# A second weight matrix read in pieces for each tile, more buffers for activations, residual and probabilities, and q ahead of o in an attention and LoRA kernel

## The chip, the core and the metric

The kernel runs on one core of one Trainium2 chip. Its engines are TensorE (PE in the profile, with its weight loads as PEld), VectorE (DVE), ScalarE (ACT), GpSimd (POOL) and SyncE (SP), which here only issues DMAs. Each has a queue of its own that it works off in order, and waits on semaphores for the others. The metric is the device time of one execution in microseconds (us).

## What is computed

The input x has 4 sequences of 512 tokens with 1024 features, in float32. Two blocks follow each other, each with a layer norm in front, a layer norm behind and a residual:

```python
x = x + layernorm(attention(layernorm(x)))
x = x + layernorm(ffn(layernorm(x)))

def attention(x):            # 32 heads of 32, 8 heads of k and v, causal
    q, k, v = split(x @ w_qkv.T + b_qkv)
    q, k = rope(q), rope(k)
    scores = where(causal, q @ k.T / sqrt(32), -1e20)
    return (softmax(scores) @ v) @ w_o.T + b_o

def ffn(x):                  # a dense layer and the two best of 8 LoRA experts
    w = softmax over the two largest of x @ gate_w.T, 0 for the others
    low = x @ lora_A[e].T    # 16 numbers for each expert
    return x @ base_w.T + base_b + 2 * sum_e w[e] * low[e] @ lora_B[e].T
```

## The kernel before

The 2048 tokens make 16 tiles of 128. A tile's position in its sequence is i = 0 to 3; its tokens attend to i + 1 blocks of 128 keys. Tile 12 (i = 0 of the last sequence) gives its k and v in its turn, but its q, attention and ffn come last of all (`line`, L584; job "12q", L586). All weights are loaded once and stay in SBUF: w_qkv, w_o, w_gl (gate and lora_A side by side), w_base, w_lora (lora_B).

For each tile the work is this.

- `load_x` (L591) loads x in two halves into the one buffer "xa"; `qkv` (L628) normalises it, turns it with TensorE (pt_xn) into T_xn, and multiplies: kv (8 steps over the 1024 features), q in two halves of 512 columns (8 steps each). A step of 512 columns is one product of 128x128 by 128x512, which the profile shows as two MATMULs. k and q are rotated (`rotated`, L506) and turned (pt_k, pt_q).
- Attention goes by groups of up to 4 heads for each of the 4 row quadrants of the array (`Group`, L1000; i = 0, 1, 2, 3 make 2, 4, 8, 8 groups for a tile). `scores` (L1011) fills one PSUM tile sc; VectorE adds the mask and takes the maximum (L1079, L1089), ScalarE takes the exponential (L1039), VectorE the reciprocal of its sum (L1048), GpSimd multiplies by it (L1053). `turn` (L1098) turns the four probability tiles (pt_p) and has them copied to prT; `values` (L1116) multiplies them by v (av). The result is put together in aT.
- `attention_out` (L768) multiplies aT by w_o (acc_o, two halves of 8 steps), adds b_o into w, normalises it, adds it to y (x of the same tile, loaded again by `load_y`, L613), and normalises y into w once more: that is h.
- `ffn` (L874) turns h (pt_h, T_h), multiplies by w_gl (acc_gl), weighs the experts (`gate`, L832), turns their 128 numbers (pt_low), and multiplies by w_base and w_lora (acc_f: two halves of 8 + 1 steps). Bias, norm and residual follow, and y goes out in two halves (L949).

What sets the order of the instructions on each engine is a planner in Python that runs while the kernel is built (`Order`, L89). It keeps an estimated time for every operation. Chains (Python generators) yield operations for VectorE, ScalarE, GpSimd or SP with a duration and an urgency (0 first); `_next` (L138) takes the most urgent that is ready, and one that is more urgent and will be ready within half the operation's time is waited for. TensorE's work stands in lanes (`tensor`, L232): the scores, the transposes of xn, h, q, k and low, the lane of pt_p and values, and the dense lanes (q and kv, o, gl and f of each tile). `_choice` (L198) takes the first lane, in this order, whose next step is ready. Among dense lanes those that have begun go first (`lane[0].bank` is false once a product has its PSUM bank), then they go in the order of the list, which L1224 to L1236 builds: for n = 0, 1, ... o of tile n-2, q and kv of tile n, then gl and f of tile n-2.

Buffers are `Slots` (L50): a chain asks for one and goes on when one is given back. The ones that the change touches:

```python
BANKS, SOFT = 4, 8
soft_slots, act_slots = Slots(SOFT), Slots(3)
xa_slots, y_slots, w_slots = Slots(1), Slots(1), Slots(2)
```

`act_slots` (three buffers "actT") hold T_xn from before its transposes to the end of q, aT from q's arrival to the end of o, and T_h from the first half of h to the end of f. T_xn also waits until the tile before it in `line` has taken its aT (`job.after`, L1192). `soft_slots` hold the probabilities pr and prT. `y_slots` has one buffer, which is given back when y has gone out to HBM; the last tile's y lies in the buffer "xa" instead, once the last x is turned (L665). All loads and stores are issued by SP in the planner's order, the weights in the sequence of `all_loads` (L1150), where w_base comes after w_o and w_gl in 8 chunks of 512 KB.

The last tile's two attention groups g0 and g1 are placed by hand (L1203 to L1205): g1 at the very end, g0 three places before the end of the list at that time, with two groups of tile 15 and then g1 behind it.

Of the kernel before, what the change touches and what calls it, by code (L numbers as in the profile page):

```python
# [11 lines left out]
F32 = mybir.dt.float32  # L12
# [4 lines left out]
P = 128  # L17
# [6 lines left out]
QUADS = P // HD  # L24
# [64 lines left out]
class Order:  # L89
# [48 lines left out]
    def _next(self):  # L138

        best = None  # L140
        for e in self.ENGINES:
            ops = self.waiting[e]
            if not ops:
                continue
            start = max(self.free[e], min(op.ready for op in ops))
            op = min(
                (op for op in ops if op.ready <= start + 1e-9), key=lambda op: (op.urgent, op.seq)
            )
            us = op.on[e][0]
            sooner = [  # L150
                o for o in ops if o.urgent < op.urgent and o.ready < start + us / 2
            ]
            if sooner:
                op = min(sooner, key=lambda o: (o.ready, o.seq))
                start = max(self.free[e], op.ready)
            if best is None or start < best[0]:
                best = (start, e, op)
        return best
# [101 lines left out]
def kernel(  # L260
# [26 lines left out]
    QSCALE = 1.0 / math.sqrt(HD)  # L287
    BANKS, SOFT = 4, 8

    const = ctx.enter_context(tc.tile_pool(name="const", bufs=1))  # L290
    xpool = ctx.enter_context(tc.tile_pool(name="xpool", bufs=1))
    acts = ctx.enter_context(tc.tile_pool(name="acts", bufs=3))
    ropes = ctx.enter_context(tc.tile_pool(name="ropes", bufs=1))
    qpool = ctx.enter_context(tc.tile_pool(name="qpool", bufs=3))
    kvpool = ctx.enter_context(tc.tile_pool(name="kvpool", bufs=3))
    soft = ctx.enter_context(tc.tile_pool(name="soft", bufs=SOFT))
    small = ctx.enter_context(tc.tile_pool(name="small", bufs=2))
    ps_sc = ctx.enter_context(tc.tile_pool(name="ps_sc", bufs=1, space=PSUM))
# [4 lines left out]
    banks = Slots(BANKS)  # L303
    soft_slots, act_slots = Slots(SOFT), Slots(3)
    qT_slots, kT_slots, raw_slots, turn_slots = Slots(3), Slots(3), Slots(2), Slots(1)
    xa_slots, y_slots, w_slots = Slots(1), Slots(1), Slots(2)
    order = Order(banks)
# [47 lines left out]
    wgl_sb = const.tile([P, ND, GL], F32, name="wgl_sb")  # L355
    wbase_sb = const.tile([P, ND, D], F32, name="wbase_sb")
    wlora_sb = const.tile([P, D], F32, name="wlora_sb")
# [21 lines left out]
    def loads(what):  # L379


        def lands(name):
            yield LANDS
            loaded[name].finish(order.at)

        for name, kb, out, in_ in what:
            yield sp(kb / RATE, lambda: nc.sync.dma_start(out=out, in_=in_))
            start(lands(name), order.at)


# [88 lines left out]

    def project(lhsT, w_sb, at, n, name, needs, take, more=None):  # L480

# [4 lines left out]
        def issue(c):  # L486
            if not acc:
# [4 lines left out]
                lhsT=lhsT()[:, c, :] if c < ND else more[0](),  # L492
                rhs=w_sb[:, c, at : at + n] if c < ND else more[1][:, at : at + n],
                start=(c == 0),
# [96 lines left out]
    def load_x(job):  # L591
# [5 lines left out]
        rows = slice(job.tok.t * P, (job.tok.t + 1) * P)  # L597
        job.xn = xpool.tile([P, D], F32, tag="xa", name=f"xa_{job.name}")

# [13 lines left out]
    def load_y(tok):  # L613

        last = tok.last
        yield (xa_slots if last else y_slots).take()
        yield has_wqkv

        def issue():
            tag = "xa" if last else "y"  # L620
            tok.y = xpool.tile([P, D], F32, tag=tag, name=f"y_{tok.t}")
            nc.sync.dma_start(out=tok.y, in_=x[tok.t * P : (tok.t + 1) * P, :])

        yield sp(P * D * 4 / 1024 / RATE, issue)
        yield LANDS
        tok.has_y.finish(order.at)

    def qkv(job, has_k, has_q):  # L628
# [33 lines left out]
        def free_x():  # L662
            yield [s.done for s in turns]
            xa_slots.give(order.at)
            if job is jobs[-1]:  # L665
                start(load_y(line[-1]), order.at)

# [80 lines left out]
        if has_k:  # L748
            products += project(
                xnT, wqkv_sb, D, 2 * KVD, f"kv_{t}", needs(D, 2 * KVD), take_kv  # L750
            )
            turned.append(step_k)
        if has_q:
            for h in range(NH):
                products += project(
                    xnT,
                    wqkv_sb,
                    h * 512,
                    512,
# [8 lines left out]
    def attention_out(tok):  # L768
# [52 lines left out]
        for h in range(NH):  # L821
# [5 lines left out]
            steps += project(  # L827
                lambda: tok.aT, wo_sb, h * 512, 512, f"o_{t}_{h}", needs, partial(take, h)
            )
# [44 lines left out]
    def ffn(tok):  # L874
# [81 lines left out]
        def rest():  # L956
# [7 lines left out]
            yield out_halves  # L964
            if not tok.last:
                y_slots.give(order.at)

        start(rest())

        def needs(name, at, more=()):  # L970
            return [
                [ready[c // 4]] + ([loaded[name, at, c]] if not t else []) for c in range(ND)
            ] + list(more)

        gl = project(
            hT,
            wgl_sb,
            0,
            GL,
# [3 lines left out]
        )  # L983
        f = [
            project(
                hT,
                wbase_sb,
                n * 512,
                512,
                f"f_{t}_{n}",  # L990
                needs("base", 0, [[tok.low_done] + ([loaded["lora"]] if not t else [])]),
                partial(take, n),
                more=(lambda: tok.lowT, wlora_sb),
            )
            for n in range(NH)
        ]
        return turns, gl + f[0][:ND] + f[1][:2] + f[0][ND:] + f[1][2:], [step_low]
# [13 lines left out]
    def scores(g):  # L1011
# [18 lines left out]

        def quadrant(r):
            yield soft_slots.take()
            pr = soft.tile([P, GROUP, P], F32, tag="soft", name=f"pr_{g.name}_{r}")
            pr = g.pr[r] = pr.rearrange("p a b -> p (a b)")
            for c in range(g.n):
                yield act(
                    0.42 + n * 0.00092,
                    1,
                    lambda: nc.scalar.activation(  # L1039
# [9 lines left out]
            for c in range(g.n):  # L1049
                yield pool(  # L1050
                    0.3 + n * 0.00085,
                    1,
                    lambda: nc.gpsimd.tensor_scalar(  # L1053
# [93 lines left out]

    has_wk, has_wqkv = Task(), Task()

    def all_loads():  # L1150
# [7 lines left out]
        for c in range(ND):  # L1158
# [6 lines left out]
            ]  # L1165
            + chunks("base", wbase_sb, w_base, 0, D)
            + [
# [5 lines left out]
        def chain():  # L1173
# [5 lines left out]
            has_wqkv.finish(order.at)  # L1179
            yield from loads(late)  # L1180

        start(chain())
# [6 lines left out]
    for n, job in enumerate(jobs):  # L1189
        at = line.index(job.tok) if job.has_q else n  # L1190

        job.after = line[at - 1] if at > 2 else line[0] if at == 2 else None  # L1192
        start(load_x(job))
    for tok in line[:-1]:
        start(load_y(tok))
# [7 lines left out]
    *groups, g0, g1 = groups  # L1203
    groups.insert(len(groups) - 0, g1)
    groups.insert(len(groups) - 3, g0)  # L1205
    for k, g in enumerate(groups):
# [17 lines left out]
    for n in range(T + 2):  # L1224

        if n > 1:
            dense_lanes.append(attention_out(line[n - 2]))
        while n < T and left and (left[0].tok.t <= line[n].t or n == T - 1):
# [3 lines left out]
            dense_lanes.append(dense)  # L1232
        if n > 1:
            turns, dense, turn_low = ffn(line[n - 2])
            turn_lanes += [turns, turn_low]
            dense_lanes.append(dense)  # L1236
    order.tensor(score_lane, turn_lanes, value_lane, dense_lanes)

# [76 lines left out]
```

## Time and profile before

| what | value |
|---|---|
| time, 3 runs | 1246.52 us median (1245.53 to 1246.68) |
| the profiled execution | 1246.57 us, of it 1244.7 us from the first to the last instruction |
| TensorE's granted clock, mean | 0.991 |
| acc_f, matmuls with w_base | 512 MATMULs 128x512, 236.0 us busy, mean 593 ns |
| acc_o | 512 MATMULs 128x512, 233.2 us busy, mean 593 ns |
| pt_p | 1280 MATMULs, 178.9 us busy; idle before them 13.5 us |
| DMA, whole execution | 44.69 MB, mean 36 GB/s |
| w_base loads | 8 of 512 KB, 9.8 us from issue to landing (median) |

"Busy" is the time in which an engine had at least one instruction under way; MATMULs are pipelined, so that their own durations overlap, and 12 of 128x512 take 5.15 us together. "Idle before" is the time in which the engine had nothing under way ahead of such an instruction, and its releaser is the instruction that ended the wait. In the slices the span is cut into 40 equal parts, with the busy share in tenths. In a table of stages each engine's busy time is followed by its number of instructions. "PEq" or "SPq" is an engine's queue.

### The profile page before, as it was taken

Reading aid. Unit: us, or ns where it says so; the run is one execution under the profiler, and the core shown is the slowest. Engines: PE = TensorE matmul, PEld = TensorE weight load, DVE = VectorE, ACT = ScalarE, POOL = GpSimd, SP = SyncE. Lnnn points to the kernel's source line nnn. Section 1 sums busy time; section 2 is a strip of 40 time slices with the busy share of each in tenths; the row PEclk is TensorE's granted clock in tenths of the full one; section 3 lists DMA queues with packets and bytes.
Section 4 is the critical chain, followed back from the end, with each engine's and each line's share of the span. In section 5 each row is a group of like instructions: output and inputs, shape, how many; then the busy total and the mean of one; then the engine's idle time right before and its main releaser. Section 6 shows DMA issues by size and latency. Waiting matters only on the chain.

```text
span 1244.7 us, 19839 instructions
## 1 busy us (share of the span) xinstructions
PE 1212.1 (97%) x7416; PEld 659.6 (53%) x7416; DVE 807.8 (65%) x1678; ACT 430.2 (35%) x1355; POOL 450.6 (36%) x696
## 2 busy tenths in 40 slices
PE   6999999999999999999999999999999999987997
PEld 3555545555555555555555555555555555544553
DVE  3657657668566766767656766667566676566653
ACT  0343433433444343433322323334433333343300
POOL 1343434143352433435332524324334242334311
PEclk9999999999999999999999999999999999997999
DMA  9800000010010101000100101010010010100000
GB/s 335 319 2 18 1 35 18 2 51 1 18 35 1 52 1 35 18 25 11 35 17 18 35 1 51 2 51 18 1 52 1 1 52 1 52 1 1 15 20 34
DMA packets 18655, 44.69 MB, mean 36 GB/s; under 512 B 2432, under 2 KB 3456, under 8 KB 18560
## 3 DMA queue, kind: packets, MB, share of 16 engines
q1 hardware_dynamic: 18560, 43.43, 9.9%
q8 instruction: 59, 0.97, 0.3%
q14 instruction: 36, 0.29, 0.1%
HBM read 35.03 MB, written 8.39 MB: 35 GB/s over the span
## 4 chain that ended last, share of the span: by engine, by line
PE 96%; DVE 2%; ACT 0%; POOL 0%; DMA 0%; issue 0%; POOLq 0%; SPq 0%; ACTq 0%
PE acc_f L490 20%; PE acc_o L490 18%; PE acc_q L490 17%; PE pt_p L1103 12%; PE acc_kv L490 9%; PE sc L1019 7%; PE av L1126 6%; PE acc_gl L490 2%; PE pt_h L465 1%; PE pt_q L721 1%; PE pt_xn L465 1%; DVE nmax L1089 0%; PE pt_k L690 0%; ACT pr L1039 0%; DMA xa<-in_x_dram 0%; DVE stats L405 0%
## 5 line engine op out<-in xcount | busy, mean ns | idle before, releaser
L1053 POOL TENSOR_SCALAR pr<-pr,rtot 128x256 f32<-128x256 f32 (+3 forms) x512 | 283.9, 572 | 405.0 <-DVE rtot L1048 369.7
L1039 ACT ACTIVATE pr<-sc,nmax 128x256 f32<-128x256 f32 (+3 forms) x512 | 263.6, 535 | 155.9 <-DVE nmax L1089 124.1
L490 PE MATMUL acc_f<-wbase_sb,T_h 128*128 128x512 f32 x512 | 236.0, 593 | 0.2 <-ACT prT L326 0.2
L490 PE MATMUL acc_o<-wo_sb,aT 128*128 128x512 f32 x512 | 233.2, 593 | 0.0
L490 PE MATMUL acc_q<-wqkv_sb,T_xn 128*128 128x512 f32 x480 | 223.1, 594 | 0.0
L326 ACT COPY prT<-pt_p 128x512 f32<-128x512 f32 (+1 forms) x193 | 103.7, 548 | 284.3 <-PE pt_p L1103 283.3
L1103 PEld LDWEIGHTS pt_p<-ident,pr 128*128 128x128 f32 x1280 | 148.4, 142 | 88.8 <-issue 64.4
L1103 PE MATMUL pt_p<-ident,pr 128*128 128x128 f32 x1280 | 178.9, 277 | 13.5 <-POOL pr L1053 13.0
L1089 DVE TENSOR_REDUCE nmax<-sc 128x4 f32<-128x1536 f32 (+5 forms) x98 | 185.6, 1894 | 9.7 <-ACT pr L1039 8.7
L327 DVE COPY prT<-pt_p 128x512 f32<-128x512 f32 (+1 forms) x159 | 101.8, 642 | 64.3 <-PE pt_p L1103 62.3
L490 PEld LDWEIGHTS acc_o<-wo_sb,aT 128*128 128x128 f32 x512 | 92.5, 190 | 94.0 <-issue 92.0
L490 PEld LDWEIGHTS acc_f<-wbase_sb,T_h 128*128 128x128 f32 x512 | 90.7, 190 | 83.6 <-issue 82.2
L490 PEld LDWEIGHTS acc_q<-wqkv_sb,T_xn 128*128 128x128 f32 x480 | 84.5, 190 | 75.2 <-issue 73.5
L490 PE MATMUL acc_kv<-wqkv_sb,T_xn 128*128 128x512 f32 x256 | 118.0, 598 | 0.7 <-DVE veps L417 0.3
L421 POOL TENSOR_TENSOR rstd<-veps,neg_half 128x1 f32<-128x1 f32 x64 | 35.6, 558 | 202.5 <-DVE veps L417 171.7
L1039 ACT ACTIVATION_READ_ACCUMULATOR pr<-sc,nmax 128x1 f32 x512 | 108.8, 212 | 0.0
L1079 DVE TENSOR_TENSOR sc<-sc,cmask 128x512 f32<-128x512 f32 (+3 forms) x98 | 83.8, 855 | 18.7 <-PE sc L1019 18.0
L1019 PE MATMUL sc<-kT,qT 32*128 32x384 f32 (+3 forms) x1024 | 95.8, 472 | 0.0
L447 POOL TENSOR_TENSOR y<-y,w 128x512 f32<-128x512 f32 x60 | 79.3, 1334 | 39.2 <-DVE w L432 38.6
L1126 PEld LDWEIGHTS av<-prT,v 128*32 128x32 f32 x2560 | 64.8, 109 | 53.1 <-issue 42.3
L1126 PE MATMUL av<-prT,v 128*32 128x128 f32 x2560 | 88.9, 276 | 0.2 <-DVE prT L327 0.2
L1048 DVE RECIPROCAL rtot<-total 128x1 f32<-128x1 f32 (+2 forms) x352 | 51.9, 156 | 52.8 <-ACT pr L1039 50.7
(83 smaller groups left out, 899.2 us busy)
## 6 DMA issues: line engine op xcount, KB each, us to landing
xa<-in_x_dram SPq DMA_DIRECT2D x32, 256.0 KB, 3.0
y<-in_x_dram SPq DMA_DIRECT2D x16, 512.0 KB, 3.6
out_dram<-y SPq DMA_DIRECT2D x32, 256.0 KB, 2.0
wqkv_sb<-in_w_qkv_dram SPq DMA_DIRECT2D x8, 512.0 KB, 8.9
wo_sb<-in_w_o_dram SPq DMA_DIRECT2D x8, 512.0 KB, 8.7
wbase_sb<-in_w_base_dram SPq DMA_DIRECT2D x8, 512.0 KB, 9.8
wqkv_sb<-in_w_qkv_dram SPq DMA_DIRECT2D x8, 256.0 KB, 5.2
bqkv_sb<-in_b_qkv_dram SPq DMA_DIRECT2D x1, 768.0 KB, 7.7
```

What stands on the lines that cost most here:

```text
L326: act=(0.15 + n * 0.00085, lambda: nc.scalar.copy(out(), in_())),
L327: dve=(0.15 + n * 0.00105, lambda: nc.vector.tensor_copy(out(), in_())),
L447: engine.tensor_tensor(out=y()[:, cols], in0=y()[:, cols], in1=z()[:, cols], op=ALU.add)
L490: nc.tensor.matmul(acc[0][:, :n], lhsT=lhsT()[:, c, :] if c < ND else more[0](), rhs=w_sb[:, c, at : at + n] if c < ND else more[1][:, at ...
L1019: nc.tensor.matmul(sc[:, r, c * n : (c + 1) * n], lhsT=tok.qT[g.kt][rows, (g.at + c) % GROUP, :], rhs=seq.kT[g.kt][rows, :n], start=True, ...
L1039: lambda: nc.scalar.activation(pr[:, c * n : (c + 1) * n], sc4[:, r, c, :], AF.Exp, bias=nmax[:, r, c : c + 1], accum_out=total[:, r, c : ...
L1048: yield dve(0.17, 1, lambda: nc.vector.reciprocal(rtot[:, r, : g.n], total[:, r, : g.n]))
L1053: lambda: nc.gpsimd.tensor_scalar(pr[:, c * n : (c + 1) * n], pr[:, c * n : (c + 1) * n], rtot[:, r, c : c + 1], 1.0, ALU.mult, ALU.mult,),
L1079: lambda: nc.vector.tensor_tensor(out=diag, in0=diag, in1=cmask.unsqueeze(1).unsqueeze(1).to_broadcast([P, q, g.n, P]), op=ALU.add,),
L1089: lambda: nc.vector.tensor_reduce(nmax[:, some, : g.n], sc4[:, some], AX.X, ALU.max, negate=True),
L1103: nc.tensor.transpose(pt[:, j, :], g.pr[r][:, j * P : (j + 1) * P], ident)
L1126: nc.tensor.matmul(av[r * HD : (r + 1) * HD, c, :], lhsT=g.seq.v[j][:, head * HD : (head + 1) * HD], rhs=g.prT[r][:, c * (i + 1) + j, :], ...
```

## The change

- w_base no longer lies in SBUF as a whole (32 KB of each partition). Eight buffers of [128, 512] (16 KB together) form a ring (`Stream`). Each ffn asks for its 16 pieces of 256 KB, 8 chunks of features for each half of the columns, in the order in which the steps use them; a buffer is given back when the step that read it is done, and SP then loads the next piece. The stream begins when all other weights are issued.
- `acts` and `act_slots` grow from 3 to 4, `soft` from 8 to 10, y from 1 to 2 buffers, of which the last tile's y now uses one too.
- T_xn of a tile waits for the aT of the tile two places before it in `line`, no longer for the one just before it.
- In the list of dense lanes, q and kv of tile n come ahead of o of tile n-2.
- The exponentials and the multiplications by the reciprocal get the urgency 1 + r / 4 for quadrant r, where it was 1 for all; in the rule that waits for a more urgent operation the fraction is cut off.
- g0 comes one place later: one group of tile 15 and then g1 stand behind it.

```diff
             sooner = [
-                o for o in ops if o.urgent < op.urgent and o.ready < start + us / 2
+                o for o in ops if o.urgent < int(op.urgent) and o.ready < start + us / 2
             ]
...
     QSCALE = 1.0 / math.sqrt(HD)
-    BANKS, SOFT = 4, 8
+    BANKS, SOFT, RING = 4, 10, 8
...
     xpool = ctx.enter_context(tc.tile_pool(name="xpool", bufs=1))
-    acts = ctx.enter_context(tc.tile_pool(name="acts", bufs=3))
+    acts = ctx.enter_context(tc.tile_pool(name="acts", bufs=4))
     ropes = ctx.enter_context(tc.tile_pool(name="ropes", bufs=1))
...
     soft = ctx.enter_context(tc.tile_pool(name="soft", bufs=SOFT))
+    weights = ctx.enter_context(tc.tile_pool(name="weights", bufs=RING))
     small = ctx.enter_context(tc.tile_pool(name="small", bufs=2))
...
     banks = Slots(BANKS)
-    soft_slots, act_slots = Slots(SOFT), Slots(3)
+    soft_slots, act_slots = Slots(SOFT), Slots(4)
     qT_slots, kT_slots, raw_slots, turn_slots = Slots(3), Slots(3), Slots(2), Slots(1)
-    xa_slots, y_slots, w_slots = Slots(1), Slots(1), Slots(2)
+    xa_slots, y_slots, w_slots = Slots(1), Slots(2), Slots(2)
     order = Order(banks)
...
     wgl_sb = const.tile([P, ND, GL], F32, name="wgl_sb")
-    wbase_sb = const.tile([P, ND, D], F32, name="wbase_sb")
     wlora_sb = const.tile([P, D], F32, name="wlora_sb")
...
             start(lands(name), order.at)
+    def part(w_sb, at, n):
+        return lambda c: w_sb[:, c, at : at + n]
+    class Stream:
+        class Piece:
+            def __init__(self, stream, in_):
+                self.stream, self.in_, self.here = stream, in_, Task()
+            def used(self, done):
+                yield done
+                self.stream.slots.give(order.at)
+        def __init__(self, w, n):
+            self.w, self.n, self.slots, self.pieces = w, n, Slots(n), []
+        def ask(self, c, cols):
+            piece = self.Piece(self, self.w[c * P : (c + 1) * P, cols])
+            self.pieces.append(piece)
+            return piece
+        def run(self, after):
+            def lands(piece):
+                yield LANDS
+                piece.here.finish(order.at)
+            yield after
+            for k, piece in enumerate(self.pieces):
+                yield self.slots.take()
+                def issue():
+                    piece.sb = weights.tile([P, 512], F32, tag="piece", name=f"piece_{k}")
+                    nc.sync.dma_start(out=piece.sb, in_=piece.in_)
+                yield sp(P * 512 * 4 / 1024 / RATE, issue)
+                start(lands(piece), order.at)
+    base_stream = Stream(w_base, RING)
...
-    def project(lhsT, w_sb, at, n, name, needs, take, more=None):
+    def project(lhsT, w, n, name, needs, take, more=None):
...
                 lhsT=lhsT()[:, c, :] if c < ND else more[0](),
-                rhs=w_sb[:, c, at : at + n] if c < ND else more[1][:, at : at + n],
+                rhs=w(c) if c < ND else more[1],
                 start=(c == 0),
...
         rows = slice(job.tok.t * P, (job.tok.t + 1) * P)
-        job.xn = xpool.tile([P, D], F32, tag="xa", name=f"xa_{job.name}")
+        job.xn = xpool.tile([P, D], F32, tag="xa", bufs=1, name=f"xa_{job.name}")
...
-        last = tok.last
-        yield (xa_slots if last else y_slots).take()
+        yield y_slots.take()
         yield has_wqkv
...
         def issue():
-            tag = "xa" if last else "y"
-            tok.y = xpool.tile([P, D], F32, tag=tag, name=f"y_{tok.t}")
+            tok.y = xpool.tile([P, D], F32, tag="y", bufs=2, name=f"y_{tok.t}")
             nc.sync.dma_start(out=tok.y, in_=x[tok.t * P : (tok.t + 1) * P, :])
...
             xa_slots.give(order.at)
-            if job is jobs[-1]:
-                start(load_y(line[-1]), order.at)
...
             yield out_halves
-            if not tok.last:
-                y_slots.give(order.at)
+            y_slots.give(order.at)
         start(rest())
-        def needs(name, at, more=()):
-            return [
-                [ready[c // 4]] + ([loaded[name, at, c]] if not t else []) for c in range(ND)
-            ] + list(more)
...
             hT,
-            wgl_sb,
-            0,
+            part(wgl_sb, 0, GL),
             GL,
...
         )
-        f = [
-            project(
+        f = []
+        for n in range(NH):
+            cols = slice(n * 512, (n + 1) * 512)
+            chunks_n = [base_stream.ask(c, cols) for c in range(ND)]
+            wants = [[ready[c // 4], chunks_n[c].here] for c in range(ND)]
+            wants.append([tok.low_done] + ([loaded["lora"]] if not t else []))
+            steps = project(
                 hT,
-                wbase_sb,
-                n * 512,
+                lambda c, chunks_n=chunks_n: chunks_n[c].sb,
                 512,
                 f"f_{t}_{n}",
-                needs("base", 0, [[tok.low_done] + ([loaded["lora"]] if not t else [])]),
+                wants,
                 partial(take, n),
-                more=(lambda: tok.lowT, wlora_sb),
+                more=(lambda: tok.lowT, wlora_sb[:, cols]),
             )
-            for n in range(NH)
-        ]
+            for c in range(ND):
+                start(chunks_n[c].used(steps[c].done))
+            f.append(steps)
         return turns, gl + f[0][:ND] + f[1][:2] + f[0][ND:] + f[1][2:], [step_low]
...
         def quadrant(r):
+            urgent = 1 + r / QUADS
             yield soft_slots.take()
...
                     0.42 + n * 0.00092,
-                    1,
+                    urgent,
                     lambda: nc.scalar.activation(
...
                     0.3 + n * 0.00085,
-                    1,
+                    urgent,
                     lambda: nc.gpsimd.tensor_scalar(
...
-    has_wk, has_wqkv = Task(), Task()
+    has_wk, has_wqkv, has_all = Task(), Task(), Task()
...
             ]
-            + chunks("base", wbase_sb, w_base, 0, D)
             + [
...
             yield from loads(late)
+            has_all.finish(order.at)
...
-        job.after = line[at - 1] if at > 2 else line[0] if at == 2 else None
+        job.after = line[at - 2] if at > 1 else None
         start(load_x(job))
-    for tok in line[:-1]:
+    for tok in line:
         start(load_y(tok))
...
     *groups, g0, g1 = groups
-    groups.insert(len(groups) - 0, g1)
-    groups.insert(len(groups) - 3, g0)
+    groups.append(g1)
+    groups.insert(len(groups) - 2, g0)
     for k, g in enumerate(groups):
...
-        if n > 1:
-            dense_lanes.append(attention_out(line[n - 2]))
         while n < T and left and (left[0].tok.t <= line[n].t or n == T - 1):
...
         if n > 1:
+            dense_lanes.append(attention_out(line[n - 2]))
             turns, dense, turn_low = ffn(line[n - 2])
...
             dense_lanes.append(dense)
+    start(base_stream.run(has_all))
     order.tensor(score_lane, turn_lanes, value_lane, dense_lanes)
```

More of the change, by code (lines that the diff above doesn't have):

```diff
@@ L749, in qkv @@
             products += project(
-                xnT, wqkv_sb, D, 2 * KVD, f"kv_{t}", needs(D, 2 * KVD), take_kv
+                xnT, part(wqkv_sb, D, 2 * KVD), 2 * KVD, f"kv_{t}", needs(D, 2 * KVD), take_kv
             )
@@ L756, in qkv @@
                     xnT,
-                    wqkv_sb,
-                    h * 512,
+                    part(wqkv_sb, h * 512, 512),
                     512,
@@ L827, in attention_out @@
             steps += project(
-                lambda: tok.aT, wo_sb, h * 512, 512, f"o_{t}_{h}", needs, partial(take, h)
+                lambda: tok.aT,
+                part(wo_sb, h * 512, 512),
+                512,
+                f"o_{t}_{h}",
+                needs,
+                partial(take, h),
             )
```

## The prediction

> **What bounds the kernel now.** I read the page's head and slices first.
>
> ```profile
> span 1244.7 us, 19839 instructions
> PE 1212.1 (97%) x7416; PEld 659.6 (53%) x7416; DVE 807.8 (65%) x1678; ACT 430.2 (35%) x1355; POOL 450.6 (36%) x696
> ...
> PE   6999999999999999999999999999999999987997
> ...
> PEclk9999999999999999999999999999999999997999
> ```
>
> TensorE is the bound, and the change keeps its matmuls: the same products, transposes, scores and values. So the time can move only in two places: in TensorE's idle time, 1244.7 - 1212.1 = 32.6 us, and in the time in which its clock is reduced. The first slice and the last four hold nearly all of it. TensorE's waits say which:
>
> ```profile
> PE pt_p L1103 <- POOL pr L1053: 13.0, 3, 8.1
> PE pt_xn L465 <- DVE xa L432: 9.5, 2, 7.7
> ```
>
> The second row is the start (x must land and be normalised); the change leaves the single xa buffer and the first loads alone. The end, after the last matmul at 1236.8, is 7.9 us of the last norm; it stays too. What is left is the first row. The stages around it (busy per engine, then granted clock, DMA share, GB/s):
>
> ```profile
> 1114.80:1119.20 4.40, 0.02 (x3) 0.00 (x0) 2.62 (x5) 1.88 (x6) 0.67 (x1) 0.78 0.00 0
> 1119.20:1121.30 2.10, 2.02 (x9) 1.44 (x9) 1.81 (x6) 1.28 (x4) 1.57 (x4) 0.50 0.00 0
> 1121.30:1123.30 2.00, 2.00 (x33) 1.79 (x32) 1.21 (x3) 0.00 (x0) 1.34 (x3) 0.50 0.00 0
> 1123.30:1124.70 1.40, 1.40 (x14) 1.22 (x10) 0.34 (x1) 0.00 (x0) 1.11 (x1) 0.72 0.00 0
> 1124.70:1126.80 2.10, 1.87 (x33) 1.06 (x32) 2.09 (x3) 0.00 (x0) 0.00 (x0) 1.00 0.00 0
> 1126.80:1134.80 8.00, 0.00 (x0) 0.00 (x0) 5.44 (x7) 4.37 (x24) 1.62 (x3) 0.76 0.00 0
> 1134.80:1136.80 2.00, 1.53 (x4) 0.74 (x5) 1.18 (x6) 1.71 (x10) 2.00 (x6) 0.50 0.01 4
> 1136.80:1141.60 4.80, 4.80 (x22) 2.97 (x22) 2.85 (x5) 0.59 (x1) 4.09 (x12) 0.55 0.01 3
> ```
>
> Idle: 4.38 + 0.08 + 0.23 + 8.00 + 0.47 = 13.2 us. After each hole the clock is at half, so busy time is stretched: 2.02x0.50 + 2.00x0.50 + 1.40x0.28 + 1.53x0.50 + 4.80x0.45 = 5.3 us. The hole costs **18.5 us**. Why no dense product filled it, the timelines show, TensorE's first:
>
> ```profile
> 1112.78 1.02 PE L490 MATMUL acc_o<-wo_sb,aT 128*128 128x512 f32 x2
> 1113.74 1.08 PE L1126 MATMUL av<-prT,v 128*32 128x128 f32 x32
> 1119.28 2.09 PE L1103 MATMUL pt_p<-ident,pr 128*128 128x128 f32 x8 [4.46 <-POOL pr L1053]
> ```
>
> At 1113.7 o of tile 14 ends. The q of the last tile has just been spent (1080 to 1098), f of the tile before ended at 1068.5, o of the next tile needs all its attention, and f of tile 14 needs its h. That h is slow because VectorE serves softmax (urgency 1) before norms (2):
>
> ```profile
> 1122.08 0.53 DVE L432 TENSOR_SCALAR w<-w,mv,rstd 128x512 f32<-128x512 f32 x1
> ...
> 1131.74 0.54 DVE L432 TENSOR_SCALAR w<-w,mv,rstd 128x512 f32<-128x512 f32 x1
> ```
>
> The second half of one normalisation comes 9.7 us after the first. From o's end to pt_h at 1136.8 are 23 us. What is short is the store of dense work, not an engine.
>
> **The change part by part.**
>
> *Fourth activation buffer, lookahead by two tiles, q ahead of o, second y buffer.* With three buffers xn of tile n+2 gets one only when hT of tile n-1 goes back: the last tile's pt_xn is at 1072.8, right after f's end at 1068.5. With four it can be turned while that hT is held, so q runs in the pause between o and f, and an f (32 + 4 matmuls at 0.429 us = 15.4 us, with gl 17.3 us) stays for later. Attention gets its q earlier where it now waits for one: sc at 613.6, the next at 651.8, where groups of three or four blocks follow each other by 10 to 12 us. So some 17 us of dense work, at best a whole o more (13.7 us), lie ready when the hole would come: more than 13.2 us. It is gone if the lead is lost. Value: -18.5 us, bounds 0 and -18.5. The second y removes a wait for output and load (out 2.0 us, y 3.6 us landing), which TensorE's waits do not show: 0. Of the moved q every instruction counts (matmuls, add, rotation, pt_q, copy), but all are only earlier; the x load ahead of q moves up on SP, past outputs, and a wait of it there would hold the pieces behind it.
>
> *w_base by pieces.* 16 tiles x 16 pieces of 256 KB are 67.1 MB in place of 4.2 MB, so 44.7 becomes 107.6 MB, 87 GB/s on average. A piece serves one step of two matmuls, 0.858 us: 262144 B / 0.858 us = 305 GB/s while an f runs undisturbed. The nearest rows: x halves of the same 256 KB and 2 KB rows, and two stages of the start, in which chunks of this shape are queued:
>
> ```profile
> xa<-in_x_dram SPq DMA_DIRECT2D x32, 256.0 KB, 3.0
> ...
> 4.00:6.00 2.00, 0.00 (x0) 0.00 (x0) 0.79 (x3) 0.00 (x0) 0.00 (x0) 1.00 0.86 303
> 6.00:8.00 2.00, 0.28 (x2) 0.28 (x3) 1.22 (x4) 0.00 (x0) 0.56 (x1) 1.00 0.94 330
> ```
>
> 303 to 330 GB/s make 0.79 to 0.87 us for a piece: rate and need are about equal. Eight buffers are the cover: piece k+8 is asked for at the end of step k and needed seven steps, 6.0 us, later; issue (0.4 us, SP's first x load took 0.37) and landing (3.0) leave 2.6 us. Between f's of two tiles q, o and attention run for tens of us, and eight pieces wait filled. The bad end: with no cover at all, TensorE follows chunks as in the first kv product, 16 matmuls in 7.91 us (0.494 against 0.429 each), so at most 0.13 us more for a step, 33 us for 256. No gain is possible, since w_base now never makes TensorE wait. A wait that is already met costs nothing visible: tile 0's f waits for its w_base chunks and runs 12 matmuls in 5.15 us, 0.429 each. I take 0.
>
> A rule speaks against the pieces. The Trainium skill, "SBUF — State Buffer", section "The DMA setup-cost knee", wants transfers coalesced and gives 224 GB/s for one of 256 KiB: 1.17 us a piece, 18.7 us for the 16 of an f of 15.4 us, 3.3 us x 16 = 53 us slower. That is the rate of transfers made one at a time. Here several are in flight, and the start shows 303 to 330 GB/s; the row decides.
>
> New waits on SP: a piece waits for the matmul that frees its buffer, and queued behind it are x loads, y loads and outputs. The planner sets a piece in SP's order when it expects the buffer, so this wait is only as long as plan and chip differ; x and y are needed tens of us later. The reverse is worse: pieces behind an output that waits for its y (GpSimd). Outputs come about 5 us after an f, when the next f's first eight pieces are already asked for. 256 issues x 0.4 us = 102 us of SP's span. I take 0; bounds 0 and the price below.
>
> *Softmax buffers 8 to 10, quadrants in order, last groups reordered.* The pt_p waits outside the hole are 0.4 us in all; 68 of 88 scores are already directly followed by values. Worth -2 to +2 us, taken as 0. SP's initial loads lose 4.2 MB of w_base, needed only at 147 us and landed near 60: 0. y of the second tile loads 512 KB ahead of w_o, needed at 92: 0.
>
> Sum: -18.5. I keep 2 us back for small holes that a new order brings (62 to 375 us hold 1.5 us of such now). Against the profiled execution's own 1246.57 us: 1246.57 - 18.5 + 2 = 1230.1; the runs' median 1246.52 gives **1230.0**.
>
> **Rivals.**
> 1. *The hole moves to the end* (18%). If attention gets so far ahead that o of tile 15 runs before f of tile 14, these two tiles' f's follow each other, o of the last tile comes late, and only its own f is left, behind its norms. That chain took from 1200.5 (w add) to 1208.5 (first half of h): 8.0 us idle, then half clock as after the 8.0 us hole above (0.77 + 2.16): 11 us. 1246.5 - 18.5 + 11 = 1239. For: dense lanes go in tile order, o's of the last tiles share two w. Against: the last 51 us now run with 0.4 us idle.
> 2. *The store is only half enough* (10%): the 8 us hole and its clock stay, the first goes: 4.4 + 0.3 + 2.4 = 7 us saved, 1239; the other way 1235.
> 3. *It does not reach the tail* (6%): the planner spends the fourth buffer on something else; 1246.
> 4. *Slower: the pieces land too late* (9%). The cover ends at a landing of 6.0 - 0.4 = 5.6 us; what is above is paid twice per tile, 32 times. It outweighs 18.5 us from 6.2 us on. x halves landed in 9.0 us at worst, in the full queue of the start; at 7 us: 32 x 1.4 = 45 less 18.5, about 1273. Against: the median of 3.0 us and a queue that is otherwise near empty.
> The main case has 57%.
>
> **The numbers.** Faster by over 0.2% (below 1244; 2.5 us is about what a measurement can tell from no change) are the main case and rivals 1 and 2: 0.85. Within it 0.06, slower 0.09. Low end: 18.5 and the small waits (1.5 + 1.9 at the start) gone with 2 us more for the order: 1224 rounded up to 1224.5; high end above rivals 1 and 2 by 2 us, 1242.
>
> **What would show it.** Right: pt_p's wait for POOL falls from 13.0 us to near 0, the clock stays at full until the last matmul, TensorE's busy sum falls by about 5 us, acc_f still takes 0.429 us a matmul with no wait for DMA, pieces land in 3 to 4 us. Wrong: acc_f rows with idle before them released by a DMA (rival 4), a hole in front of pt_h after 1190 us (rival 1), a pt_p hole of some 8 us (rival 2).

## The result and the profile after

The changed kernel took 1243.79 us (median of 8 runs, 1240.62 to 1244.43) against 1246.49 us before: a ratio of 0.9974, 95% interval 0.9964 to 0.9985. The forecast was 1230.0 us, with a range of 1224.5 to 1242 us. The direction was right; only 2.7 of the 16.5 us came, and the time lies outside the range.

The page of the changed kernel's profiled execution (1241.56 us), the same rows as were read before:

```profile
span 1239.8 us, 20306 instructions
...
PE 1210.3 (98%) x7416; PEld 658.6 (53%) x7416; DVE 809.4 (65%) x1673; ACT 434.6 (35%) x1360; POOL 455.5 (37%) x696
...
PE   7999999889999999999999999999999999999997
```

TensorE's idle time fell from 32.6 us only to 29.5 us. But it is no longer where it was: the last slices are full, and slices 8 and 9 (217 to 279 us), full before, have each lost about a tenth. TensorE's waits, and the busy time of each engine in the stages around the new hole, around a second one, and at the end (then clock, DMA share, GB/s):

```profile
PE pt_p L1143 <- ACT prT L327: 2.9, 4, 0.8
PE pt_p L1143 <- DVE rtot L1088: 2.7, 3, 0.9
PE pt_p L1143 <- POOL pr L1093: 2.6, 2, 2.0
```

```profile
237.70:244.80 7.10, 4.01 (x23) 2.40 (x19) 4.77 (x8) 3.64 (x10) 1.50 (x3) 0.92 0.23 77
244.80:248.60 3.80, 3.27 (x41) 1.39 (x40) 1.86 (x5) 0.00 (x0) 1.24 (x2) 0.70 0.01 4
248.60:254.50 5.90, 2.51 (x16) 1.68 (x16) 3.64 (x7) 3.86 (x10) 1.36 (x2) 0.95 0.00 0
254.50:257.70 3.20, 3.18 (x4) 1.42 (x5) 0.10 (x2) 0.00 (x0) 1.36 (x2) 0.56 0.03 1
...
916.30:922.00 5.70, 3.07 (x54) 2.21 (x54) 4.09 (x12) 0.27 (x1) 3.46 (x5) 1.00 0.01 3
922.00:926.30 4.30, 4.30 (x11) 2.07 (x10) 4.23 (x9) 0.59 (x1) 3.16 (x7) 0.61 0.00 0
1100.00:1232.00 132.00, 129.33 (x725) 69.88 (x723) 79.53 (x186) 36.19 (x122) 41.53 (x67) 1.00 0.42 132
```

The last row is the old place, at full clock: up to the last matmul, which ends at 1231.6, 2.3 us are idle where 18.5 us had been lost. The first four rows are a new hole. Its idle time is 3.09 + 0.53 + 3.39 + 0.02 = 7.0 us, and the reduced clock stretches its busy time by 4.01x0.08 + 3.27x0.30 + 2.51x0.05 + 3.18x0.44 = 2.8 us. At 916 us come 2.6 us idle and 4.30x0.39 = 1.7 us of clock. With a wait of 0.4 us at 227 the new holes take back 9.8 + 0.4 + 4.3 = 14.5 of the 18.5 us.

The balance of the two profiled executions: up to the last matmul TensorE's idle time fell by 3.4 us (24.7 to 21.3) and the time lost to the reduced clock by 0.8 us (5.3 to 4.5), the last norm took 0.3 us longer, and 1.0 us less was spent busy at full clock. Together that is the 4.9 us by which the spans differ. The 1.0 us may be cheaper changes between kinds of matmul (84 of 88 scores are now directly followed by values, 68 before), but no run tested it.

The runs between 1240.6 and 1244.4 follow the granted clock: 1240.62 and 1241.56 us at a mean of 0.995, 1242.61 at 0.993, the other five, 1243.46 to 1244.43, at 0.991. So the profiled run is one of the better ones, and the median is 2.2 us above it, in runs with a lower clock.

What TensorE does in the new hole, from its timeline:

```profile
237.69 1.12 PE L531 MATMUL acc_f<-piece,T_h 128*128 128x512 f32 x2
238.65 0.27 PE L957 MATMUL pt_low<-ident,low 128*128 128x128 f32 x1
239.37 0.63 PE L1143 MATMUL pt_p<-ident,pr 128*128 128x128 f32 x4 [0.45 <-ACT lowT L327]
240.82 0.63 PE L1143 MATMUL pt_p<-ident,pr 128*128 128x128 f32 x4 [0.82 <-ACT prT L327]
...
253.04 0.63 PE L1143 MATMUL pt_p<-ident,pr 128*128 128x128 f32 x4 [0.88 <-DVE rtot L1088]
254.52 3.37 PE L531 MATMUL acc_f<-piece,T_h 128*128 128x512 f32 x4 [0.85 <-DVE prT L328]
```

The first half of an f is complete up to its w_lora step at 238.8; then for 15.7 us no dense product runs, though the pieces that f needs next have landed (SP asked for them from 230.8 us on, and the DMA share falls to near 0). Each pt_p waits until the copy before it has read its PSUM bank, and starts 0.14 us after it, as if one bank were left (where the line names rtot, VectorE had ended a copy to prT just before). VectorE's timeline says why. A product gives its bank back when VectorE adds the bias into a raw buffer. The last matmuls of a q half and of a kv, and VectorE's additions:

```profile
215.35 1.02 PE L531 MATMUL acc_q<-wqkv_sb,T_xn 128*128 128x512 f32 x2
224.58 1.88 PE L531 MATMUL acc_kv<-wqkv_sb,T_xn 128*128 128x512 f32 x4
...
206.53 0.68 DVE L556 TENSOR_TENSOR raw_q<-acc_q,bqkv_sb 128x512 f32<-128x512 f32 x1
...
265.75 0.68 DVE L556 TENSOR_TENSOR raw_q<-acc_q,bqkv_sb 128x512 f32<-128x512 f32 x1
266.87 0.43 DVE L556 TENSOR_TENSOR raw_k<-acc_kv,bqkv_sb 128x256 f32<-128x256 f32 x1 [0.44 <-PE pt_q L758]
```

The addition at 206.5 is that of the q half before. The q half whose last matmul ends at 216.4 is added at 265.8, the kv that ends at 226.5 at 266.9: their banks were held for 49 and 40 us. With f's first half that makes three of four banks, and the pt_p, whose lane comes before the dense ones, go on taking the fourth. f's second half needs a bank of its own before the first half can end (the order of steps in `ffn`'s last line), so the lane of f stands still. The two raw buffers are taken by a k that waits for kT of the sequence before (added at 152.3, turned at 264.3) and a q half that waits for room in qT (added at 206.5, turned at 266.2). In the kernel before one bank was held in this place, from 216.8 to 256.0 (39 us), and 217 to 260 us had 0.6 us of waits:

```profile
213.22 3.60 PE L490 MATMUL acc_q<-wqkv_sb,T_xn 128*128 128x512 f32 x8
...
255.98 0.68 DVE L515 TENSOR_TENSOR raw_q<-acc_q,bqkv_sb 128x512 f32<-128x512 f32 x1
```

### The profile page after: what moved, and what is told of

Same layout as the page of the kernel before. It is cut to its first block, busy times and chain, and to the rows that moved or that the text cites. A ratio compares the mean times of both kernels' runs of the same rounds, so it can differ in the third digit from the quotient of the medians.

```text
span 1239.8 us, 20306 instructions
## 1 busy us (share of the span) xinstructions
PE 1210.3 (98%) x7416; PEld 658.6 (53%) x7416; DVE 809.4 (65%) x1673; ACT 434.6 (35%) x1360; POOL 455.5 (37%) x696
## 4 chain that ended last, share of the span: by engine, by line
PE 95%; DVE 2%; ACT 1%; POOL 1%; issue 0%; DMA 0%; POOLq 0%; SPq 0%; ACTq 0%; DVEq 0%
PE acc_f L531 20%; PE acc_q L531 17%; PE acc_o L531 17%; PE pt_p L1143 12%; PE acc_kv L531 9%; PE sc L1058 7%; PE av L1166 6%; PE acc_gl L531 2%; PE pt_xn L505 1%; PE pt_h L505 1%; PE pt_q L758 1%; ACT pr L1079 1%; DVE nmax L1129 0%; PE pt_k L727 0%; DVE prT L328 0%
## 5 line engine op out<-in xcount | busy, mean ns | idle before, releaser
L1093 POOL TENSOR_SCALAR pr<-pr,rtot 128x256 f32<-128x256 f32 (+3 forms) x512 | 288.6, 577 | 519.5 <-DVE rtot L1088 426.6
L531 PE MATMUL acc_f<-piece,T_h 128*128 128x512 f32 x512 | 236.5, 597 | 2.3 <-ACT prT L327 1.4
L531 PEld LDWEIGHTS acc_f<-piece,T_h 128*128 128x128 f32 x512 | 91.7, 191 | 90.8 <-issue 84.8
## 6 DMA issues: line engine op xcount, KB each, us to landing
piece<-in_w_base_dram SPq DMA_DIRECT2D x256, 256.0 KB, 3.4
xa<-in_x_dram SPq DMA_DIRECT2D x32, 256.0 KB, 3.0
out_dram<-y SPq DMA_DIRECT2D x32, 256.0 KB, 2.0
wqkv_sb<-in_w_qkv_dram SPq DMA_DIRECT2D x8, 256.0 KB, 5.1
```

What stands on the lines that cost most here:

```text
L531: nc.tensor.matmul(acc[0][:, :n], lhsT=lhsT()[:, c, :] if c < ND else more[0](), rhs=w(c) if c < ND else more[1], start=(c == 0), stop=last,)
L1093: lambda: nc.gpsimd.tensor_scalar(pr[:, c * n : (c + 1) * n], pr[:, c * n : (c + 1) * n], rtot[:, r, c : c + 1], 1.0, ALU.mult, ALU.mult,),
```

## The experiments

Theory A: q and kv now run so early that their accumulators hold PSUM banks, and this makes the new hole. Theory B: there is simply no dense work in that place. Theory C: the pieces of w_base cost the time. Theory D was formed after the first four runs: the end depends on the exact order of TensorE's work, apart from banks. A ratio is against the kernel before, run beside it on the same chip. There its median was 1246.3 to 1247.3 us, so differences between kernels of different series are good to about 1 us.

**e1: a third raw buffer in the changed kernel.**

```diff
-    qT_slots, kT_slots, raw_slots, turn_slots = Slots(3), Slots(3), Slots(2), Slots(1)
+    qT_slots, kT_slots, raw_slots, turn_slots = Slots(3), Slots(3), Slots(3), Slots(1)
-        raw = ropes.tile([P, 512], F32, tag="raw", bufs=2, name=f"raw_{name}")
+        raw = ropes.tile([P, 512], F32, tag="raw", bufs=3, name=f"raw_{name}")
-                seq.v[i] = kvpool.tile([P, KVD], F32, tag="v", bufs=6, name=f"v_{t}")
+                seq.v[i] = kvpool.tile([P, KVD], F32, tag="v", bufs=8, name=f"v_{t}")
```

> The changed kernel with three raw buffers in place of two (and eight v buffers in place of six, without which the deeper lookahead has no place for v). Theory A (PSUM banks): the new hole at 237 to 255 us comes from the accumulators of an early q half and of an early kv, which hold two of four banks for 50 and 41 us because both raw buffers are taken by a k and a q that wait for room in kT and qT. With a third raw buffer one of the two banks is given back at once, f's second half gets its bank, and most of the 7.4 us of idle time and 2.8 us of clock there go: 1233 to 1237 us. Theory B (the store of dense work is empty there, whatever the banks): the hole stays, 1243 us. Theory C (reading w_base in pieces costs the time): 1243 us, hole unchanged.

Measured: 1256.28 us, ratio 1.0072 (1.0057 to 1.0087). Two stages of its profile, and its longest wait:

```profile
210.00:270.00 60.00, 59.25 (x372) 31.79 (x370) 38.96 (x82) 22.56 (x60) 21.65 (x29) 1.00 0.27 88
1100.00:1245.00 145.00, 124.54 (x660) 66.98 (x648) 77.82 (x174) 29.71 (x110) 37.75 (x64) 0.92 0.32 105
```

```profile
1224.12 1.97 PE L505 MATMUL pt_h<-ident,w 128*128 128x128 f32 x8 [7.91 <-DVE w L472]
```

A is right on the hole: the q half gives its bank back at once, the kv still holds one for 35 us, and the stage has 0.75 us of idle time left. Theory B falls with it, since dense work was there to fill the place. A is wrong on the time: 20.5 us of idle time and a clock of 0.92 come at the end. The 7.9 us in front of pt_h have the place and size of the prediction's first rival, though o of tile 15 did not run before f of tile 14: the second half of the last tile's o runs (1209 to 1216) after f of tile 15, and its norms stand alone.

**e2: a fourth kT buffer in the changed kernel** (`kvpool` bufs 3 to 4, `kT_slots` to 4, v to 8).

> The changed kernel with a fourth kT buffer (and eight v buffers): k of the first tile of a sequence no longer waits in a raw buffer for the sequence before. Theory A: the raw buffer that k held from 152 to 264 us is free, the q half and the kv behind it leave their banks at once, the hole goes as with a third raw buffer or more fully: 1232 to 1236 us. Theories B and C: 1243 us.

Measured: 1260.10 us, 1.0102 (1.0087 to 1.0117). The same as e1: no idle time between 210 and 270 us, no hold over 12 us, but TensorE waits 16.5 us after 1100 us, 7.9 of them in front of pt_h, and 5 us between 960 and 1100. A's time is missed again.

**e3: o ahead of q again in the changed kernel** (`attention_out` appended ahead of the `while` loop).

> The changed kernel with o of tile n-2 ahead of q and kv of tile n again, all else as changed. Theory A: q and kv run less early, so their accumulators hold banks for less time; the hole at 237 us shrinks, while the fourth activation buffer still keeps a store for the end: 1234 to 1240 us. If q ahead of o is what filled the hole of before at 1113 us, that hole comes back: 1246 to 1252 us.

Measured: 1248.05 us, 1.0009 (1.0002 to 1.0015). A's guess was wrong: the holds are still 52 and 43 us and the hole is whole (7.4 us idle, 210 to 270). So the order of q and o does not make the hole. It does help to fill the end: without it 6.4 us of idle time stand there, against 2.3.

**e4: x's turning tied to the tile just before** in the changed kernel.

```diff
-        job.after = line[at - 2] if at > 1 else None
+        job.after = line[at - 1] if at > 2 else line[0] if at == 2 else None
```

> The changed kernel with the turning of x tied to the tile just before again (aT of the tile one place before), all else as changed. Theory A: q and kv of the next tile come later by an attention, the long holds of banks shrink as in the kernel before (one of 39 us), the hole at 237 us goes and the hole of the end partly returns: 1238 to 1246 us. If the tie did not bind in the changed kernel: 1243 us.

Measured: 1246.88 us, 0.9998 (0.9991 to 1.0005), just above A's 1238 to 1246. The hole at 237 us is gone (0.0 us idle from 210 to 270; one hold of 17 us), and TensorE waits 12.4 us after 1100 us, 7.9 of them again in front of pt_h. So it is the lookahead by two tiles that holds the banks: two held banks made a hole in the changed kernel and in e3, one did not in the kernel before, in e1 and in e4. The later runs agree: e7, e8 and e10 also have two long holds (31 to 50 us) and 7.4 to 7.8 us idle from 210 to 270; every run with one long hold or none has at most 0.8 us.

**e5: the pieces alone**, in the kernel before.

> The kernel before with w_base read in pieces through eight buffers and nothing else of the change. Theory C (the pieces cost time): 1 to 5 us over the kernel before, with idle time in front of acc_f that a DMA ends. Theories A and D (the pieces are free, and the order of TensorE's work alone moves the time): 1246.5 us within 1 us, with the hole at 1113 us as before.

Measured: 1246.58 us, 1.0001 (0.9992 to 1.0009). Theory C falls. The rows of acc_f and of the pieces in its profile:

```profile
L531 PE MATMUL acc_f<-piece,T_h 128*128 128x512 f32 x512 | 236.0, 593 | 0.2 <-ACT prT L327 0.2
...
piece<-in_w_base_dram SPq DMA_DIRECT2D x256, 256.0 KB, 3.2
```

236.0 us and 593 ns are the numbers of the resident w_base, to the digit. 63 MB more are read, and no matmul waits for a piece, here or in the changed kernel.

**e6: e4 with g0 six places before the end.**

```diff
-    groups.insert(len(groups) - 2, g0)
+    groups.insert(len(groups) - 6, g0)
```

> The changed kernel with x's turning tied to the tile just before again, as in e4, and the last tile's first group g0 six places before the end of the list in place of two. Theory D: the tie removes the holds of PSUM banks and with them the hole at 237 us, as e4 showed, and what e4 gave back at the end (an 8 us hole in front of pt_h) depends on when the last tile's groups let their o run; with g0 earlier o of the last tile comes sooner, that hole goes, and both savings are kept: 1230 to 1237 us. If the end must starve whenever the start does not (one store of work, spent once): 1244 to 1250 us.

Measured: 1232.94 us, 0.9889 (0.9875 to 0.9902). Theory D holds: 0.0 us idle from 210 to 270, 1.8 us after 1100. Both savings can be had together. What is left is a hole of 3.6 us in front of pt_h at 908 us, beside a kv that holds its bank for 5.3 us, and its clock.

Only g0 moved between e4 and e6, and this shows what the hole in front of pt_h was. The end of e4, then that of e6:

```profile
1173.74 4.12 PE L531 MATMUL acc_o<-wo_sb,aT 128*128 128x512 f32 x8
1177.70 0.60 PE L505 MATMUL pt_h<-ident,w 128*128 128x128 f32 x4
1182.01 2.02 PE L531 MATMUL acc_gl<-wgl_sb,T_h 128*128 128x136 f32 x16
1199.42 7.03 PE L531 MATMUL acc_o<-wo_sb,aT 128*128 128x512 f32 x16
1214.35 1.97 PE L505 MATMUL pt_h<-ident,w 128*128 128x128 f32 x8 [7.90 <-DVE w L472]
...
1170.00 13.14 PE L531 MATMUL acc_o<-wo_sb,aT 128*128 128x512 f32 x30
1182.98 0.60 PE L505 MATMUL pt_h<-ident,w 128*128 128x128 f32 x4
1186.43 2.02 PE L531 MATMUL acc_gl<-wgl_sb,T_h 128*128 128x136 f32 x16
```

In e4 h of tile 15 is turned (pt_h at 1177.7) during the first half of the last tile's o. The second half would need a new bank, so it does not count as begun, and gl and f of tile 15, which stand ahead of it in the list, are served first. When the second half ends, only the last tile's own f is left, and that waits for its norms. In e6 the last o follows o of tile 15 directly, both of its halves run before gl, and f of tile 15 covers the norms.

**e7: four buffers for the pieces** in the changed kernel (`RING = 4`).

> The changed kernel with four buffers for w_base's pieces in place of eight. A piece is then asked for three steps, 2.6 us, ahead; issue and landing (0.4 + 3.4 us in the changed kernel's profile) are 1.2 us longer. If nothing else filled these gaps, 1.2 us for every four pieces, 77 us in all. The planner knows of the landing and puts attention and other products between, so 1246 to 1265 us. If landing doesn't matter even so: 1243 us.

Measured: 1249.99 us, 1.0022 (1.0013 to 1.0031), 6.2 us over the changed kernel. Now TensorE waits for the pieces:

```profile
PE acc_f L531 <- DMA piece<-in_w_base_dram: 4.2, 9, 1.1
```

9 waits of up to 1.1 us are near the 1.2 us of the sum; that they are 9 and not 64 says how much work the planner puts between. acc_f's busy time grew by 10.4 us (236.5 to 246.9), so some of the waiting may be counted as busy; the 6.2 us are not split further, since the order changed as well.

**e8: g0 back at three places before the end** in the changed kernel.

> The changed kernel with g0 three places before the end, as in the kernel before, all else as changed. If this place sets what is left at the end, a hole of some 4 us comes back after 1100 us: 1245 to 1250 us; if not: 1243 us. The hole at 237 us stays in both.

Measured: 1252.23 us, 1.0040 (1.0026 to 1.0054): one place of one group is worth 8.4 us, more than the forecast for the hole that it brings (5.3 us in front of pt_h, 6.9 us of waits in all after 1100, and clock).

**e9: e6 with three activation buffers** (`acts` and `act_slots` back to 3).

> The kernel of e6 (tie to the tile just before, g0 six places before the end) with three activation buffers, as before the change, in place of four. If the fourth buffer is what keeps a store of dense work for the end, a hole in front of pt_p or pt_h of some 10 us comes back after 1100 us: 1245 to 1252 us. If e6 owes its time to the tie, the order and g0 alone: 1233 us.

Measured: 1247.24 us, 1.0001 (0.9992 to 1.0009). The fourth buffer is worth 14.3 us in e6. Without it pt_p waits 5.6 us for GpSimd after 1100 us. The store for the end is only part of the 14.3: of the 13.2 us between the two profiled executions 4.4 are idle time after 1100, and less than 1 is idle time elsewhere (more from 100 to 880, less around 908). Some 8.4 us are busy time, of which the longer time at half clock (10.2 against 3.4 us) explains at most 3.4. The other 5 are not explained; only 60 of 88 scores are directly followed by values, against 79 in e6.

**e10: one y buffer** in the changed kernel, with the last tile's y in "xa".

> The changed kernel with one y buffer, and the last tile's y in the x buffer, as before the change. The prediction put the second y at 0: 1243 us. If h of a tile has to wait for the output of the tile before it whenever f's are held back for the end, as the fourth activation buffer makes them be, a hole in front of pt_h or pt_p comes at the end: 1250 to 1262 us.

Measured: 1256.37 us, 1.0084 (1.0066 to 1.0102): the second y is worth 12.6 us. GpSimd's addition to y waits 5.3 us for y's load, which SP issues at 1194.5, after the output at 1191.2, and TensorE then waits 2.9 us in front of pt_h. 12.8 us are idle in all after 1100. The longest hole there is no wait for y: 6.5 us in front of pt_p at 1130 to 1138, before this load, which came with the new order.

**e11: e6 with a third raw buffer** (and eight v buffers, as in e1).

> The kernel of e6 with a third raw buffer and eight v buffers. In e6 one q half still holds a PSUM bank for 17 us at 241 us without idle time around it; if only such holds with idle time cost anything, 1231 to 1233 us, as e6. If each hold delays attention, some us less: 1226 to 1230 us.

Measured: 1227.33 us, 0.9841 (0.9827 to 0.9854), the best version: 16 us less than the changed kernel, 20 less than the one before. The page and TensorE's waits (the two long ones; the next is 0.8 us):

```profile
span 1225.7 us, 20332 instructions
...
PE   7999999999999999999999999999999999999997
```

```profile
PE pt_xn L505 <- DVE xa L472: 8.6, 2, 7.0
PE pt_h L505 <- DVE w L472: 1.1, 1, 1.1
```

Only the start and the last norm still have long waits. No q or kv accumulator is held over 3 us, and the 3.6 us hole at 908 us has gone with the hold beside it.

**e12 and e13: e11 with the tie two places back, and e11 with o ahead of q.**

> The kernel of e11 with the tie to the tile two places before, as in the change. If the two places cost only through the held PSUM banks, the third raw buffer has cured that: 1226 to 1231 us, no hole. If the deeper lookahead of itself leaves the end worse provided, as e1 hints, a hole after 1100 us comes: 1245 to 1252 us.

> The kernel of e11 with o of tile n-2 ahead of q and kv of tile n, as before the change. If q ahead of o is what builds the store for the end, holes after 1100 us come back: 1246 to 1262 us. If the fourth activation buffer and the second y do that alone: 1227 to 1232 us.

Measured: e12 1246.12 us, 0.9993 (0.9985 to 1.0002); e13 1258.27 us, 1.0094 (1.0078 to 1.0111). With a third raw buffer e12 has no hole at 237 us (0.75 us idle), and still TensorE waits 12.8 us after 1100, 7.9 of them in front of pt_h. So the deeper lookahead costs by its order too, not by banks alone: 19 us here. And q ahead of o, worth 4 us in the changed kernel (e3), is worth 31 us in e11. Without it 15.7 us are idle after 1100, again 7.9 of them in front of the last pt_h.

## Why the prediction was wrong

- **Where the time could come from.** Right: TensorE's matmuls did not change, and idle time and clock account for the difference within 1 us.
- **The hole at 1113 us, -18.5 us.** Right in the kernel as a whole: after 1100 us 2.3 us of idle time are left, at full clock, and f products run from 1111 to 1125, where the hole had been. The fourth activation buffer (e9, 14.3 us) and q ahead of o (e13, 31 us) are needed for it, as the step said, though only part of e9's 14.3 us lies at the end. The lookahead by two tiles, which the prediction counted to the same cause, was not needed for it: e6 and e11 fill the end without it.
- **The moved q. This step failed.** The prediction said of its instructions that "all are only earlier" and gave them no price. An earlier q or kv takes its PSUM bank earlier and gives it back only when a raw buffer is free, which hangs on kT and qT of the attention before. Two banks held made a hole of 9.8 us (7.0 idle, 2.8 clock), shown by e1, e2 and e4, which take away a hold in three ways and with it the hole. The sum kept 2 us for all such holes; the profile has 9.8 + 0.4 + 4.3 = 14.5. The trace of the kernel before had the warning: a q half that held its bank for 39 us from 217 on. The second hole, at 916 us, lies beside a kv held for 6.2 us; no run took it away alone, so its cause is argued.
- **The second y at 0.** Wrong: 12.6 us in the changed kernel (e10). It was read from the waits of the kernel before. In the new order an addition does wait for its y, 5.3 us in e10; the rest of the 12.6 lies in holes that came with the new order, and is not settled.
- **Softmax buffers, quadrants and g0 within 2 us.** Wrong for g0's place alone: 8.4 us (e8). No run took away the two softmax buffers or the quadrants' order, so their share is not known.
- **The pieces at 0.** Right: e5, 1.0001. The 53 us, an estimate from the 224 GB/s that the Trainium skill gives in "SBUF — State Buffer", "The DMA setup-cost knee", do not appear. The pieces overlap: from 318.8 us on SP issued 16 of them in 18.8 us, 1.2 us each, while one took 3.4 us (median) from issue to landing, against 3.0 in the sum. e7 shows that the cover was needed: with four buffers TensorE waits.
- **The rivals.** The hole of the first, 8.0 us in front of the last pt_h, did not come in the changed kernel, but came in e1, e2, e4, e12 and e13 with 7.9 us, by another order than the rival's (e6). The hole that did come in the changed kernel was in none of them: they all looked at the end and at the DMAs.
- **Two slips in the working** do not move the argument. The idle time of the kernel before lies in the first slice and the last five, not four. The low end's terms, taken as written, give 1246.5 - 18.5 - 1.5 - 1.9 - 2 = 1222.6, not 1224.

The traces of all runs agree on the 7.9 us hole. In the five that have it, tile 15's h is turned before the first half of the last o has ended, all 36 MATMULs of tile 15's f run between the two halves, and only the last tile's own 36 are left. In the ten others, the kernel before and the changed one among them, both halves of the last o come first and 72 are left. The changed kernel escaped this hole by 1.6 us (the first half ended at 1187.5, pt_h came at 1189.1). No step of the prediction had worked that out, so that its first rival stayed away was luck. Not settled is which orders make the other holes of the end, in front of pt_p with GpSimd as releaser (5.5 to 8.3 us in e1, e2, e3, e9 and e13).

## What to carry to other kernels

Before work is moved earlier, list everything that it holds until its consumer takes it, PSUM banks first, and follow what its evacuation waits for; an accumulator whose evacuation waits for an SBUF buffer is a bank lost for that time. When a kernel has one full engine and several buffer counts, the worth of one count is measured only beside the others: here q ahead of o was worth 4 us in one combination and 31 in another, and a third raw buffer cost 12 us in the changed kernel (e1) and gained 6 in e6 (e11). So a cure for one hole is tested with the order at the end tuned again.

## What was not expected of the hardware

The clock fell to half without any long pause. From 237.7 to 254.5 us no gap was over 1 us and TensorE was busy for 9.8 of 16.8 us, mostly in bursts of some 0.6 us; still the profile's clock records have it at half for 3.4 us, twice between 243 and 258 us (means of 0.70 and 0.56 in the rows above). The Trainium skill, "TensorE: Matmul & The Clock Gate", "A second HAM failure mode: psum-queue depth-cycling", tells of another kernel in which small pauses of TensorE between groups of matmuls, as it goes through the PSUM banks, are frequent enough to make the clock swing between half and full. This trace agrees. How much the same pauses cost is not fixed: e3, also with 7.4 us idle from 210 to 270, has 13.6 us at half clock there, the changed kernel 6.8. The 4 us between the changed kernel's runs go along with their mean clocks, 0.995 to 0.991.
